# Feed-forward groups of five blocks instead of four in a pre-norm transformer block on one Trainium2 core

## The chip, the core and the metric

The kernel runs as one program on one core of one Trainium2 chip. The metric is the time of one execution on the device in microseconds (us). Three executions of the kernel before took 2558.55, 2560.4 and 2563.48 us, so the median is 2560.4 us. The arithmetic is float32 throughout.

Engines are named as the profile names them: PE multiplies matrices (its weight loads are shown as PEld), DVE is the vector engine, ACT the scalar engine, POOL the general one, and SP is the queue that issues nearly all DMA transfers. Each engine runs its own instructions in order and waits on the others through semaphores.

## The reference

The input x has 2048 rows (tokens) of 1024. The reference computes

```
x = x + attention(layernorm(x), wq, bq, wk, bk, wv, bv)   # 32 heads of 32, attention over the heads of each token
n = layernorm(x)
h = silu(n @ dq(w1).T) * (n @ dq(w2).T)                   # w1, w2: 2752 x 1024
x = x + h @ dq(w3).T                                      # w3: 1024 x 2752
```

where `dq` quantizes a weight to the 16 NF4 levels in blocks of 64 values, scaled by each block's largest absolute value, and expands it again. So every weight of the feed-forward part has to pass through `dq` inside the kernel. The 2752 hidden features are 21 blocks of 128 and a half block of 64. The code numbers them 0 to 21.

## The kernel before, in words

**Two halves.** The first part (up to some 840 us of the profile) projects q, k and v and computes the attention, in three sweeps over eight pairs of token tiles. The second part is the feed-forward. The products are built by a Strassen-like scheme: seven products stand in for eight. On the way, sums of operand tiles are kept in DRAM.

**The dequantization runs beside all this as a background job.** The list `jobs` holds one job for each weight block: kind "1" and "2" for the rows of w1 and w2, kind "3" for the columns of w3, kind "12" for the two half blocks together. There are 65 jobs. Their order follows `GROUPS`: for each group first the jobs "1" and "2" of all its blocks, then the jobs "3" of all its blocks. The generator `background()` cuts a job into steps, 17 for each job: 15 threshold steps (an ACT instruction into `sg`, L211, and a DVE instruction into `r`, L214 or L216), a step that takes the next job's absolute maxima (`am`, L184, with 16 small ACT multiplications into `wn`, L172), and a last step that scales `r` back. Once the feed-forward runs, every second job scales with one DVE instruction (L227), the others with 16 ACT multiplications (L172). A finished job then waits in `pending` for its transposes (`finish`): PE transposes it in two halves of four (`ptw`, L146), ACT copies each half to `wop` (L147), and for kinds 2, 12 and 3 an SP transfer stores the result in DRAM (`wd`, L159).

**How steps come into the program.** The order of PE's instructions is the order in which the code emits them. The order on the other engines is chosen by the framework's scheduler from readiness and program order. In the attention part, `advance(n)` emits n steps at fixed places. In the feed-forward, each product calls `spent`, which emits 0.67 steps for each nominal microsecond of PE work, and lets `flush(1)` emit one piece of transposing when the running job has reached its sixth step or later. Where a block is needed that isn't stored yet, `until` emits steps and transposes at once, without waiting for their turn:

```
def until(kind, c):
    while (kind, c) not in wd:
        if pending:
            flush(1)
        else:
            next(bg)
```

**The feed-forward.** Tokens are handled in two halves (`tbp` 0 and 1) of 1024. A pass is one group of blocks for one half. For each block of the group a `Unit` computes seven products (`mul`, each of four 128x128 by 128x512 matmuls and `spent(3.43)`), and makes from them two tiles `h`. The products run in the order first (one), middle (four), last (two), and the first product of the next unit is put between middle and last of the present one. Block 0 of half 0 is computed earlier, beside the end of the attention, by `plain_block`. After the middle of a group's last unit, `ask_w3(g)` loads the third weights of the group's blocks from DRAM into tiles of the pool `w3p`, through `load_w3`, which first calls `until("3", c)`:

```
if unit.c == min(g[-1], NFULL - 1):
    for c in [c for c in w3T if c not in g]:
        del w3T[c]
    ask_w3(g)
```

**The sums.** Then `down` multiplies the `h` of the group with the third weights: for each of 8 token tiles of the half and 2 column halves, one sum over the group's blocks grows in a PSUM bank (`po`, L924), and one DVE addition adds it to a running sum `acc` (L945). `acc` is loaded from DRAM (`x1d`) before and stored after, by SP; the last group stores to the output. Each `down` calls `spent(1.7 * len(full))` eight times. The passes go (g0, half 0), (g0, half 1), (g1, half 1), (g1, half 0) and so on, and the third weights stay for both passes of a group.

Of the kernel before, what the change touches and what calls it, by code (L numbers as in the profile page):

```python
# [12 lines left out]
FP = mybir.dt.float32  # L13
# [5 lines left out]
P = 128  # L19
# [10 lines left out]
NFULL = F // P  # L30
HALF = F - NFULL * P
TB = 512
NTBP = S // (2 * TB)
RATE = 0.67
XOPS = ("B11", "B12", "B21", "B22", "T1", "T2", "T3", "T4")
GROUPS = [list(range(g, min(g + 4, NFULL + 1))) for g in range(0, NFULL + 1, 4)]
BIG = float(2.0**100)

NF4_CODE = np.array(
# [19 lines left out]
def preln_block_kernel(  # L59
# [51 lines left out]
    jobs = []  # L111
    for g in GROUPS:
        for c in g:
# [135 lines left out]
    left, right = ExitStack(), ExitStack()  # L249
# [504 lines left out]
        advance(n)  # L754

    def new_h():
        return hp.tile([P, TB], FP, tag="h", name="h", bufs=10)

    def plain_block(c, tbp):

# [51 lines left out]
    tail.close()  # L812

    hp = ctx.enter_context(tc.tile_pool(name="hp", bufs=1, side="left", reuse_waits="tile"))
    w3p = ctx.enter_context(tc.tile_pool(name="w3p", bufs=5, side="left", reuse_waits="tile"))
    accp = ctx.enter_context(tc.tile_pool(name="accp", bufs=3, side="left", reuse_waits="tile"))
    ps_q = ctx.enter_context(
        tc.tile_pool(name="ps_q", bufs=2, space=PSUM, side="left", reuse_waits="tile")
# [12 lines left out]
    class Unit:  # L831
# [19 lines left out]
        def middle(self):  # L851
            q = self.q = ps_q.tile([P, TB], FP, tag="q", name="q")
            self.mul(7, q, True, False)
            self.mul(6, self.z, False, False)
            u2 = self.u2 = hp.tile([P, TB], FP, tag="u2", name="u2", bufs=2)
            nc.scalar.copy(u2, self.z)  # L856
            r = ps_r.tile([P, TB], FP, tag="r", name="rr")
            self.mul(2, r, True, True)
            nc.vector.tensor_tensor(self.g0, self.g0, r, ALU.add)
            nc.scalar.activation(self.g0, self.g0, AF.Silu)  # L860
            self.mul(5, self.z, False, False)
            u4 = hp.tile([P, TB], FP, tag="u4", name="u4")
            nc.scalar.copy(u4, self.z)
            self.h = [new_h(), new_h()]
            nc.vector.tensor_tensor(self.h[1], u4, q, ALU.add)
# [11 lines left out]
    class Half:  # L877


        def __init__(self, tbp):  # L880
            until("12", NFULL)
            self.tbp = tbp
            self.w = wT.tile([P, 7, 4, P], FP, tag="w12", name="w12h")
            nc.sync.dma_start(self.w[:, 0:2], wd["12", NFULL])
            self.si = hp.tile([P, TB], FP, tag="si", name="si")
            self.h = new_h()
# [21 lines left out]
    def down(g, tbp, hs):  # L908

        full = [c for c in g if c < NFULL]  # L910
        last = g is GROUPS[-1]
        for q in range(4):
# [42 lines left out]
    passes = []  # L955
    for n, g in enumerate(GROUPS):
        for tbp in (0, 1) if n % 2 == 0 else (1, 0):
# [68 lines left out]
```

## Time and profile before

| | before |
|---|---|
| median of three executions | 2560.4 us |
| the profiled execution | 2564.3 us |
| its span in the profile | 2562.5 us |
| PE, DVE, ACT busy | 2456.5, 2001.2, 1674.9 us |
| additions `acc` (L945) | 192, mean 682 ns |
| loads of `acc` from `x1d`, stores to `x1d` | 96, 80, of 512 KB each |
| mean granted PE clock | 0.982 |

The span runs from the first to the last instruction in the profile. The time of the execution, 2564.3 us, is 1.8 us longer and lies 3.9 us above the median. In a group's line of the profile, "x1344 | 599.4, 600 | 17.2" says that there are 1344 instructions, busy for 599.4 us, of mean 600 ns, and that the engine was idle for 17.2 us just before them. PE's instructions overlap: each float32 matmul of 128x512 is two records of some 0.6 us that start 0.43 us apart, so one `mul` is eight records and 3.43 us.

### The profile page before, as it was taken

To read this page: it belongs to the slowest core of one execution; us is meant where nothing else is said; L and a number is where in the kernel's file an instruction comes from. 1 tells how busy PE (TensorE), PEld (TensorE's weight loads), DVE (VectorE), ACT (ScalarE), POOL (GpSimd) and SP (SyncE) were. 2 spreads that over 40 slices of the span, in tenths; PEclk is the share of its full clock that TensorE was granted. 3 is DMA by queue.
4 is the path that set the end of the run, shared out by engine and by line. 5 is a ranking of instruction groups with operands and counts; after the bars stand their busy time and mean duration, and the time that the engine had idled before them with its cause. 6 is when DMAs were issued, how large, how long until landed. Compare 5 with 4: busy or idle time off the path is not lost.

```text
span 2562.5 us, 36651 instructions
## 1 busy us (share of the span) xinstructions
PE 2456.5 (96%) x14160; PEld 1151.3 (45%) x14160; DVE 2001.2 (78%) x2240; ACT 1674.9 (65%) x3190; POOL 31.6 (1%) x72
## 2 busy tenths in 40 slices
PE   8999899999998999999999999999999999999997
PEld 4444455544444444444444444444444444444433
DVE  7998788878898588888888888889888898871222
ACT  4657545445654478879788898888987978861000
POOL 1000000000000000000000000000000000000000
PEclk9999999999998999999999999999999999999999
DMA  8789533646677673364643546335365253641474
GB/s 301 290 308 353 205 140 131 243 166 211 219 241 268 224 265 133 136 221 156 246 144 136 197 156 263 144 122 219 123 252 187 107 209 134 231 184 62 149 280 142
DMA packets 156849, 506.03 MB, mean 197 GB/s; under 512 B 13633, under 2 KB 67905, under 8 KB 136833
## 3 DMA queue, kind: packets, MB, share of 16 engines
q1 hardware_dynamic: 156096, 503.63, 54.3%
q8 instruction: 111, 1.82, 0.3%
q14 instruction: 66, 0.53, 0.1%
q10 hardware_dynamic: 576, 0.05, 0.0%
HBM read 317.77 MB, written 185.86 MB: 197 GB/s over the span
## 4 chain that ended last, share of the span: by engine, by line
PE 24%; DVE 20%; ACT 17%; issue 6%; DMA 1%; DVEq 0%; SPq 0%
DVE r L216 16%; PE z L311 9%; PE po L924 9%; ACT sg L211 7%; ACT wn L172 5%; PE q L311 3%; ACT r L172 3%; PE rr L311 2%; ACT wop L147 1%; DVE acc L945 1%; PE po L936 1%; PE ptw L146 1%; DVE r L214 1%; DVE r L227 0%; ACT u L856 0%
## 5 line engine op out<-in xcount | busy, mean ns | idle before, releaser
L211 ACT ACTIVATE sg<-wn 128x1024 f32<-128x1024 f32 (+1 forms) x975 | 1012.0, 1048 | 304.7 <-DVE r L216 259.9
L216 DVE SCALAR_TENSOR_TENSOR r<-sg,r 128x1024 f32<-128x1024 f32 (+1 forms) x910 | 1104.2, 1213 | 113.5 <-ACT sg L211 75.5
L924 PE MATMUL po<-w,h 128*128 128x512 f32 x1344 | 599.4, 600 | 17.2 <-DVE acc L945 14.0
L924 PEld LDWEIGHTS po<-w,h 128*128 128x128 f32 x1344 | 251.8, 192 | 338.8 <-issue 289.6
L311 PE MATMUL z<-xB,w 128*128 128x512 f32 x720 | 323.3, 598 | 14.3 <-DMA w<-wd 12.0
L311 PE MATMUL z<-xT,w 128*128 128x512 f32 x656 | 297.2, 596 | 2.0 <-ACT u L856 1.9
L311 PE MATMUL q<-xT,w 128*128 128x512 f32 x656 | 291.0, 592 | 0.0
L172 ACT ACTIVATE wn<-wn,rc 128x64 f32<-128x64 f32 x1032 | 270.4, 336 | 26.6 <-DVE rc L192 26.6
L311 PEld LDWEIGHTS z<-xB,w 128*128 128x128 f32 x720 | 134.9, 192 | 175.4 <-issue 165.0
L945 DVE TENSOR_TENSOR acc<-acc,po 128x512 f32<-128x512 f32 x192 | 129.8, 682 | 107.2 <-PE po L924 64.9
L311 PE MATMUL z<-wB,A 128*128 128x512 f32 x384 | 186.3, 631 | 17.5 <-ACT u L329 17.3
L311 PEld LDWEIGHTS q<-xT,w 128*128 128x128 f32 x656 | 123.7, 190 | 151.3 <-issue 149.4
L311 PEld LDWEIGHTS z<-xT,w 128*128 128x128 f32 x656 | 123.0, 191 | 149.7 <-issue 140.6
L311 PE MATMUL z<-wT,A 128*128 128x512 f32 x384 | 181.4, 617 | 7.1 <-ACT u L329 4.5
L311 PE MATMUL q<-wT,A 128*128 128x512 f32 x384 | 173.1, 593 | 2.4 <-DVE A L364 1.5
L172 ACT ACTIVATE r<-r,am 128x64 f32<-128x64 f32 x608 | 152.4, 338 | 27.0 <-DVE r L216 27.0
L311 PE MATMUL rr<-xB,w 128*128 128x512 f32 x328 | 150.0, 601 | 0.0
L184 DVE TENSOR_REDUCE am<-wn 128x16 f32<-128x1024 f32 (+1 forms) x65 | 78.4, 1206 | 61.1 <-ACT r L172 55.8
L311 PEld LDWEIGHTS z<-wB,A 128*128 128x128 f32 x384 | 73.6, 201 | 100.9 <-issue 78.3
L311 PEld LDWEIGHTS z<-wT,A 128*128 128x128 f32 x384 | 72.4, 195 | 89.9 <-issue 81.7
L311 PEld LDWEIGHTS q<-wT,A 128*128 128x128 f32 x384 | 71.9, 190 | 90.0 <-issue 82.9
L856 ACT COPY u<-z 128x512 f32<-128x512 f32 x41 | 23.5, 573 | 131.6 <-PE z L311 131.6
(104 smaller groups left out, 1809.8 us busy)
## 6 DMA issues: line engine op xcount, KB each, us to landing
w<-wd SPq DMA_DIRECT2D x41, 1280.0 KB, 6.9
acc<-x1d SPq DMA_DIRECT2D x96, 512.0 KB, 3.5
wd<-wop SPq DMA_DIRECT2D x21, 2048.0 KB, 6.9
x1d<-acc SPq DMA_DIRECT2D x80, 512.0 KB, 2.9
wn<-in_w_dram SPq DMA_DIRECT2D x63, 512.0 KB, 4.1
w<-wd SPq DMA_DIRECT2D x62, 512.0 KB, 4.1
xT<-xdT SPq DMA_DIRECT2D x28, 1024.0 KB, 8.0
xB<-xdB SPq DMA_DIRECT2D x24, 1024.0 KB, 4.8
```

The costliest lines, as they stand in the source:

```text
L146: nc.tensor.transpose(pt[:q, k, :], v[:, j * q : (j + 1) * q], ident)
L147: nc.scalar.copy(o[:q, first + half], pt[:q])
L172: nc.scalar.mul(dst[:, ts(n, BLOCK)], src[:, ts(n, BLOCK)], by[:, n : n + 1])
L184: nc.vector.tensor_reduce(am[:, :nb], v.rearrange("p (b e) -> p b e", e=BLOCK), AX.X, ALU.max, apply_absolute_value=True,)
L211: nc.scalar.activation(t, v, AF.Copy, bias=EDGES[i], scale=BIG)
L214: nc.vector.tensor_scalar(r, t, code, -1.0, ALU.min, ALU.max)
L216: nc.vector.scalar_tensor_tensor(r, t, code, r, ALU.min, ALU.max)
L311: nc.tensor.matmul(dst, w[:, k, :], xop[:, k, :], start=start and k == 0, stop=stop and k == 3, skip_group_check=True,)
L856: nc.scalar.copy(u2, self.z)
L924: nc.tensor.matmul(po, hs[c][j][:, ts(q, P)], w3T[c][:, ts(n, 512)], start=(c == g[0]), stop=(c == g[-1]), skip_group_check=True,)
L936: nc.tensor.matmul(po, hs[NFULL][r, ts(q, P)], w3T[NFULL][r, ts(n, 512)], start=False, stop=True, skip_group_check=True,)
L945: nc.vector.tensor_tensor(a[:, ts(n, 512)], a[:, ts(n, 512)], po, ALU.add)
```

## The change

Groups have five blocks instead of four: 0 to 4, 5 to 9, 10 to 14, 15 to 19, and 20 with the half block 21, where before they were 0 to 3, 4 to 7, 8 to 11, 12 to 15, 16 to 19, and 20 with 21. That makes five groups and ten passes instead of six and twelve. The order of the background's jobs changes with the groups. A sum in PSUM runs over five blocks. The ring of `h` tiles has 12 buffers instead of 10, and the ring of third weights 6 instead of 5.

```diff
-GROUPS = [list(range(g, min(g + 4, NFULL + 1))) for g in range(0, NFULL + 1, 4)]
+GROUPS = [list(range(g, min(g + 5, NFULL + 1))) for g in range(0, NFULL + 1, 5)]
...
     def new_h():
-        return hp.tile([P, TB], FP, tag="h", name="h", bufs=10)
+        return hp.tile([P, TB], FP, tag="h", name="h", bufs=12)
...
-    w3p = ctx.enter_context(tc.tile_pool(name="w3p", bufs=5, side="left", reuse_waits="tile"))
+    w3p = ctx.enter_context(tc.tile_pool(name="w3p", bufs=6, side="left", reuse_waits="tile"))
```

## The prediction

> **What bounds the kernel now.** I read the page first, then the waits of the stretch 960 to 2200 us, then busy time by stage, then single waits in the timelines.
>
> ```profile
> PE 2456.5 (96%) x14160; PEld 1151.3 (45%) x14160; DVE 2001.2 (78%) x2240; ACT 1674.9 (65%) x3190; POOL 31.6 (1%) x72
> DVE  7998788878898588888888888889888898871222
> ACT  4657545445654478879788898888987978861000
> L945 DVE TENSOR_TENSOR acc<-acc,po 128x512 f32<-128x512 f32 x192 | 129.8, 682 | 107.2 <-PE po L924 64.9
> ```
>
> PE is busy 96% of the span, yet DVE and ACT stand at 8 or 9 tenths from slice 15 to slice 36: the feed-forward while weights are still being dequantized. After about 2300 us only PE works. Two things can therefore set the pace: PE's program, or the chain of DVE and ACT that makes the weights. The waits from 960 to 2200 us (total, times, longest) show which:
>
> ```profile
> ACT sg L211 <- DVE r L216: 137.7, 256, 2.1
> DVE r L216 <- ACT sg L211: 62.7, 59, 3.4
> DVE am L184 <- ACT r L172: 39.5, 18, 3.8
> DVE acc L945 <- PE po L924: 16.9, 10, 3.2
> PE po L924 <- DVE acc L945: 14.0, 11, 3.4
> PE ptw L146 <- DVE r L227: 11.8, 3, 6.4
> ```
>
> DVE and ACT wait for each other, hardly for PE. The scalings of every second job, from the view of tile r in that stretch, give the chain's pace:
>
> ```profile
> L227 DVE TENSOR_TENSOR r<-r,am x23: 1217/1219/1225, 982.1 to 2195.7; 128x1024 f32<-128x1024 f32 x23
> ```
>
> That is 22 intervals of two jobs in 1213.6 us: 27.6 us a job. PE's program advances a job each 17 steps, 17 / 0.67 = 25.4 us of nominal work; its 8 transposes start 0.11 us apart and add 0.9: 26.3 us. So the chain is the slower one by 1.3 us a job, and PE loses that in small waits. PE's start-to-start times beyond the regular 0.43 and 0.11 us sum to some 26 us in the downs and 24 us in the units that have background work. The last is the clearest (PE, DVE and ACT timelines):
>
> ```profile
> 2187.11 3.60 PE L311 MATMUL z<-xT,w 128*128 128x512 f32 x8
> 2197.10 1.09 PE L146 MATMUL ptw<-ident,r 128*128 128x128 f32 x4 [6.39 <-DVE r L227]
> 2197.98 6.09 PE L311 MATMUL rr<-xB,w 128*128 128x512 f32 x8
> ```
> ```profile
> 2195.73 1.22 DVE L227 TENSOR_TENSOR r<-r,am 128x1024 f32<-128x1024 f32 x1
> ```
> ```profile
> 2167.59 3.93 ACT L172 ACTIVATE r<-r,am 128x64 f32<-128x64 f32 x16
> ```
>
> PE waits 6.39 us for job 61's scaling, which ends at 2196.95; the job before it, 60, ended at 2171.52 on ACT. From 2197.10 on PE has 365.4 us to the end of the span, no longer bound by the chain.
>
> **What the change removes.** One group less is two passes less: 32 additions of 0.682 us (21.8 us of DVE), 32 loads and 32 stores of 512 KB. PE's matmuls stay: 1344 records of po either way. One set of operand loads goes too. The DMAs are worth nothing directly: acc lands in 3.5 us, and DVE waited for it 2.0 us in the stretch. What they cover is PE's time, so I count only the additions, through the chain. The additions also hold PSUM banks that PE wants (14.0 us above, some more at the weight loads); with five blocks a pair of sums takes 8.6 us of PE instead of 6.9, so each bank has more time to come free. That belongs to the same chain and isn't counted twice. The larger rings match the group: 10 tiles of h and 2 for the next unit, 5 third weights and one spare, as 8 and 2, 4 and 1 before. No cost, unless they were smaller.
>
> **What it moves: the deadline of the last third weight.** Job k is complete at step 17k + 1. By the code the attention emits 8 x 7 + 8 x 8 + 8 x 9 = 192 steps, the plain block 3: 195.
> - Before: the first request for third weights comes after 19 products: 195 + 19 x 3.43 x 0.67 = 238 steps. Job 12 needs 205: 33 in hand. A cycle of two passes emits (56 x 3.43 + 2 x 8 x 6.8) x 0.67 = 201.6 and needs 12 x 17 = 204. So 31, 28, 26 and 24 are in hand at the next four requests, and `until` never emits anything.
> - After: the first request comes after 26 products: 195 + 59 = 254 steps. Job 15 needs 256. A cycle emits (70 x 3.43 + 2 x 8 x 8.5) x 0.67 = 252 and needs 255. So each of four requests is 2 to 3 steps short: `until` emits them and both halves of the transposes at once, in front of PE's next product. A slack of 24 to 33 steps (36 to 49 us) becomes none, four times.
>
> The parts of this wait: (a) PE stands until the job is scaled. (b) Between the two halves PE waits for ACT's copy, since `ps_tr` has one buffer; I take 2.5 us with the transposes (0.45 each), bounds 1.5 to 4: copies of 0.57 us followed the transposes by up to 2.4 us in the trace. (c) Then copy, store and load of that third weight: about 2 + 3.1 + 4.1 (the medians to landing) + 0.7 for two issues = 9.9 us, beside one product of the next unit, two of this one and 3.4 us of the first sum = 13.7 us. Covered, with 3.8 us to spare. The next unit's weights don't queue behind it: SP's order follows readiness (the trace issues a third weight as soon as it is stored, 31 us before its down). Queued behind the wait on PE is everything; on ACT the copy of the next unit's first product.
>
> **The sum.** At the first request the chain is ahead (the neighbouring job 14 was ready 14 us before PE reached its point), so only (b) counts. At the fourth, job 60 decides. The PE work left there: 3 products in the stage, a down of 20 product-lengths, 35 products, a down of 20 = 78 before the last group. At 2197.10 in the trace there are 5 + 16 + 28 + 16 = 65. The difference is 13 x 3.43 = 44.6 us. So
> end = T60 + 3.5 (release, both halves, copy) + 44.6 + 365.4 - 2.5 (the slow matmuls at 2197.98: 6.09 instead of 3.60) = T60 + 411.0.
> T60 was 2171.5. What shifts it: 32 additions less by that point (6 downs instead of 8), credit between 0 (ACT is the bound) and 21.8; I take three quarters, 16.4, because in the downs DVE is nearer to full than ACT (this stage, from the busy times by stage: DVE 52.56 and ACT 45.31 of 57.70):
>
> ```profile
> 1401.80:1459.50 57.70, 56.98 (x142) 25.14 (x141) 52.56 (x61) 45.31 (x84) 0.00 (x0) 1.00 0.56 205
> ```
>
> About 1.1 units more by then (33.7 against 32.6) x 5 DVE operations of 0.684 = +3.8. DVE and ACT starved for part of (b) at the second and third request: 0 to 4 us each, I take 1.5: +3. So T60 = 2161.9, and the end 2572.9.
> Plus the clock. After the gaps of 6.4 us here, 4.0 at 1977.1, 3.2 at 1278.7 and 3.5 at 1603.1, four to eight matmul records started 0.85 us apart instead of 0.43: 1.6 to 3.1 us lost; after one of 3.5 at 1767.7, none. One such loss lies behind the last decisive wait (earlier ones are absorbed by the next wait for the chain): +3, bounds 0 to 3.1. Span 2576, which is +13.5; from the profiled execution 2564.3 that is 2578, from the median, 3.9 lower, 2574.
>
> [...]
>
> **Range of the forecast.** Full credit, no starving, no clock loss: T60 = 2153.5, end 2564.5, +2: 2562. No credit, 4 us twice, the dearer (b) and clock: T60 = 2183.3, end 2599, +36: 2597.
>
> **Rivals.**
> 1. *Faster.* The additions are the bound, and with them gone the weights are ready when asked: the chain gains on PE. Then the waits of 26 us in downs halve, the 16 us behind late scalings (waits of 1.7, 4.0 and 6.4, and slow matmuls) go, and four times (b) is paid: -13 - 16 + 10 = -19, 2541. For it: DVE above 90% in downs. Against: ACT has the same 65 jobs and DVE waits for it 102 us. It decides if job 60 is done at or before PE arrives: PE passes that place at about 2144 before (ten products after the down that ends at 2107.5), so T60 would have to fall by 28 us; the additions hold 21.8, and the chain would have to lose its waits for PE (16.9 us) as well.
> 2. *No change.* The saving and the late deadline cancel: the low end above with some of the 26 us regained. 2560.
> 3. *Much slower.* The last third weight lands late. With the longest landings of these rows (11.7 for a store, 7.6 for a load) path (c) is 22 us, 8.2 over its cover, four times: 2574 + 33 = 2607. Against: medians of 3.1 and 4.1.
>
> **Chances.** Forecast 0.68, rival 1 0.14, rival 2 0.10, rival 3 0.08. The measurement tells 0.2%, 5 us, from no change. Of the forecast's range a small part, 0.03, lies within that: faster 0.14, same 0.13, slower 0.73. To hold 8 in 10 the range takes the forecast and rival 2, and reaches halfway to rival 3: 2559 to 2600.
>
> **What would show it.** Four PE waits at ptw, at about 930, 1340, 1750 and 2165 us, the first short, the later ones of 5 to 25 us with DVE r or ACT r as releaser, each followed by the last w3 load; 160 additions; fewer waits po <- acc; background done by about 2285; after the fourth wait PE without gaps. Wrong: if those waits are under 3 us (rival 1), or if PE waits at po for w3 loads (rival 3), or if job 60 ends after 2171.

## The result and the profile after

The change makes the kernel slower. Five executions of the kernel after gave a median of 2620.07 us (2618.62 to 2627.45), beside 2561.93 us for the kernel before in the same comparison: a ratio of 1.0239, 95% interval 1.0226 to 1.0253, or 58 us. The direction was forecast. The size, +13.5 us, was not, and 2620 lies above the range of 2559 to 2600. The profiled execution took 2620.07 us, its span is 2618.3 us (before 2562.5), the mean granted PE clock 0.972 (before 0.982).

From the profile's page of the kernel after: busy time by engine, the slices of DVE and ACT, and three groups (busy and mean ns, then the idle time just before them and what ended most of it).

```profile
PE 2466.4 (94%) x14160; PEld 1160.5 (44%) x14160; DVE 1987.5 (76%) x2208; ACT 1681.1 (64%) x3190; POOL 31.7 (1%) x72
DVE  7998778889886677887888888788788788751122
ACT  4658545545444776887987797898788798751000
L945 DVE TENSOR_TENSOR acc<-acc,po 128x512 f32<-128x512 f32 x160 | 108.0, 681 | 146.4 <-PE po L924 103.5
L146 PE MATMUL ptw<-ident,r 128*128 128x128 f32 (+1 forms) x520 | 89.3, 291 | 70.5 <-DVE r L227 31.5
L147 ACT COPY wop<-ptw 128x512 f32<-128x512 f32 (+1 forms) x130 | 74.8, 578 | 82.6 <-PE ptw L146 82.5
```

The 32 additions are gone, with the 21.8 us of DVE that were counted. The work is the same otherwise, but DVE and ACT now dip to 7 tenths and below again and again where before they stood at 8 and 9. Both lines of transposing have changed most: PE is idle 70.5 us before its transposes (L146), where before it was 12.8, and ACT 82.6 before its copies (L147; before 51.4), waiting for PE. The same two lines of the kernel before, and its ACT's wait for transposes from 960 to 2320 us:

```profile
L146 PE MATMUL ptw<-ident,r 128*128 128x128 f32 (+1 forms) x520 | 78.8, 275 | 12.8 <-DVE r L227 11.8 <-ACT wop L147 1.0
L147 ACT COPY wop<-ptw 128x512 f32<-128x512 f32 (+1 forms) x130 | 74.2, 573 | 51.4 <-PE ptw L146 51.2
ACT wop L147 <- PE ptw L146: 11.1, 5, 3.2
```

The waits of the stretch 960 to 2320 us, which holds the feed-forward with background work, show the pair in the kernel after (some lines left out):

```profile
ACT sg L211 <- DVE r L216: 149.5, 319, 1.5
DVE r L216 <- ACT sg L211: 63.6, 60, 3.2
...
DVE acc L945 <- PE po L924: 45.4, 25, 4.0
ACT wop L147 <- PE ptw L146: 38.7, 14, 8.4
...
PE ptw L146 <- DVE r L227: 31.5, 5, 10.7
PE ptw L146 <- ACT wop L147: 21.2, 7, 4.0
...
PE ptw L146 <- ACT r L172: 12.9, 11, 8.4
DVE r L214 <- PE ptw L146: 9.7, 3, 3.3
```

Two things are to be seen. `PE po <- DVE acc`, 14.0 us before, is gone: a bank does have more time to come free. And there is a loop that the kernel before did not have at this size: ACT and DVE wait for PE's transposes (`wop <- ptw`, 38.7 us where it was 11.1, and `r` L214 `<- ptw`, the first instruction of a new job, which before had no such wait after 1000 us), while PE waits for their scalings.

The timeline of PE shows how. First one down of the kernel after, then the next pass, to the place where PE stops.

```profile
1149.55 25.91 PE L924 MATMUL po<-w,h 128*128 128x512 f32 x60
1175.30 0.60 PE L146 MATMUL ptw<-ident,r 128*128 128x128 f32 x4
1175.74 8.75 PE L924 MATMUL po<-w,h 128*128 128x512 f32 x20
1184.32 0.60 PE L146 MATMUL ptw<-ident,r 128*128 128x128 f32 x4
1184.76 25.92 PE L924 MATMUL po<-w,h 128*128 128x512 f32 x60
1210.51 0.60 PE L146 MATMUL ptw<-ident,r 128*128 128x128 f32 x4
...
1259.50 3.60 PE L311 MATMUL z<-xB,w 128*128 128x512 f32 x8
1273.81 1.09 PE L146 MATMUL ptw<-ident,r 128*128 128x128 f32 x4 [10.71 <-DVE r L227]
1274.69 5.87 PE L311 MATMUL z<-xB,w 128*128 128x512 f32 x8
```

In 70 us PE transposes three halves, 1.5 jobs. DVE in the same place:

```profile
1211.37 1.23 DVE L227 TENSOR_TENSOR r<-r,am 128x1024 f32<-128x1024 f32 x1
...
1219.73 0.69 DVE L945 TENSOR_TENSOR acc<-acc,po 128x512 f32<-128x512 f32 x1 [3.60 <-PE po L924]
1223.68 0.69 DVE L214 TENSOR_SCALAR r<-sg 128x1024 f32<-128x1024 f32 x1 [3.26 <-PE ptw L146]
```

A job is scaled at 1212.60. The next one's first threshold is ready on ACT at 1212.42, but both buffers of `r` hold finished jobs, one half transposed and one not at all, so DVE can start it (L214) only at 1223.68, after the transposes at 1222.97. For 11.1 us the chain makes no threshold: DVE has 3.7 us of additions and small steps, ACT 4.5 us of a copy and of the small multiplications into `wn`. That job ends at 1249.8, 37.2 us after the one before it, and the one after that at 1273.7. PE has run out of other work at 1263.1 and waits 10.71 us for it. The chain loses 11 us in the down, where PE has plenty to do, and PE pays them in the next pass.

The cause is a count in the code; the experiments below test it. `down` calls `spent` eight times, whatever the group's size, and each call gives `flush(1)` one turn at most. With five blocks those eight calls emit 8 x 8.5 x 0.67 = 46 steps, 2.7 jobs, which need 5.4 halves of transposing; with four, 36 steps, 2.1 jobs, 4.3 halves, and three or four were transposed. The pile that was small with four blocks grows past what two buffers of `r` can hold.

### The profile page after: what moved, and what is told of

Same layout as the page of the kernel before. It is cut to its first block, busy times and chain, and to the rows that moved or that the text cites. A ratio compares the mean times of both kernels' runs of the same rounds, so it can differ in the third digit from the quotient of the medians.

```text
span 2618.3 us, 36524 instructions
## 1 busy us (share of the span) xinstructions
PE 2466.4 (94%) x14160; PEld 1160.5 (44%) x14160; DVE 1987.5 (76%) x2208; ACT 1681.1 (64%) x3190; POOL 31.7 (1%) x72
## 4 chain that ended last, share of the span: by engine, by line
PE 39%; DVE 15%; ACT 11%; issue 3%; DMA 2%; DVEq 0%; SPq 0%
PE po L924 21%; DVE r L216 12%; PE z L311 10%; PE q L311 5%; ACT sg L211 5%; ACT wn L172 3%; ACT r L172 2%; PE rr L311 2%; PE ptw L146 1%; DMA out_dram<-acc 1%; DMA acc<-x1d 1%; ACT wop L147 1%; DVE r L214 0%; DVE am L184 0%; DVE r L227 0%
## 5 line engine op out<-in xcount | busy, mean ns | idle before, releaser
L924 PE MATMUL po<-w,h 128*128 128x512 f32 x1344 | 585.9, 594 | 2.8 <-DVE h L871 2.8
L311 PE MATMUL z<-xB,w 128*128 128x512 f32 x720 | 335.3, 615 | 13.3 <-DMA w<-wd 11.9
L311 PE MATMUL q<-xT,w 128*128 128x512 f32 x656 | 298.4, 606 | 0.3 <-DVE acc L945 0.3
L172 ACT ACTIVATE wn<-wn,rc 128x64 f32<-128x64 f32 x1032 | 268.7, 336 | 37.2 <-DVE rc L192 37.2
L945 DVE TENSOR_TENSOR acc<-acc,po 128x512 f32<-128x512 f32 x160 | 108.0, 681 | 146.4 <-PE po L924 103.5
L146 PE MATMUL ptw<-ident,r 128*128 128x128 f32 (+1 forms) x520 | 89.3, 291 | 70.5 <-DVE r L227 31.5
L146 PEld LDWEIGHTS ptw<-ident,r 128*128 128x128 f32 (+1 forms) x520 | 66.7, 147 | 140.6 <-issue 45.4
L147 ACT COPY wop<-ptw 128x512 f32<-128x512 f32 (+1 forms) x130 | 74.8, 578 | 82.6 <-PE ptw L146 82.5
```

What stands on the lines that cost most here:

```text
L146: nc.tensor.transpose(pt[:q, k, :], v[:, j * q : (j + 1) * q], ident)
L147: nc.scalar.copy(o[:q, first + half], pt[:q])
L172: nc.scalar.mul(dst[:, ts(n, BLOCK)], src[:, ts(n, BLOCK)], by[:, n : n + 1])
L311: nc.tensor.matmul(dst, w[:, k, :], xop[:, k, :], start=start and k == 0, stop=stop and k == 3, skip_group_check=True,)
L924: nc.tensor.matmul(po, hs[c][j][:, ts(q, P)], w3T[c][:, ts(n, 512)], start=(c == g[0]), stop=(c == g[-1]), skip_group_check=True,)
L945: nc.vector.tensor_tensor(a[:, ts(n, 512)], a[:, ts(n, 512)], po, ALU.add)
```

## The experiments

The main theory is this pile-up: too few turns of `flush` in a down fill the ring `r` and stop the chain. Rival A is the prediction's own mechanism at a larger price: the requests for third weights that `until` forces are the loss. All ratios are to the kernel before in the same comparison, with 95% intervals. Medians come from several comparisons, in which the kernel before had 2556.3 to 2561.9 us, so runs are compared by their ratios. T60 is the time at which job 60 is scaled, as in the prediction; a job's pace is taken from job 21 to job 61.

| run | blocks | median us | ratio | T60 | us a job |
|---|---|---|---|---|---|
| before | 4 | 2560.4 (three executions) | | 2171.5 | 27.6 |
| after | 5 | 2620.1 | 1.0239 [1.0226, 1.0253] | 2198.9 | 28.1 |
| e1_after_flush | 5 | 2562.6 | 1.0007 [0.9995, 1.0018] | 2143.2 | 27.0 |
| e2_before_rare | 4 | 2643.5 | 1.0325 [1.0303, 1.0347] | 2251.6 | 29.2 |
| e3_rings | 4 | 2561.2 | 1.0004 [0.9990, 1.0018] | 2167.5 | 27.6 |
| e4_before_flush | 4 | 2561.9 | 0.9998 [0.9984, 1.0012] | 2165.7 | 27.4 |
| e5_flush_lead | 5 | 2562.8 | 1.0015 [1.0004, 1.0026] | 2127.3 | 27.1 |
| e6_lead | 5 | 2601.4 | 1.0160 [1.0140, 1.0180] | 2178.1 | 28.0 |
| e7_r3 | 5 | 2568.0 | 1.0035 [1.0022, 1.0047] | 2144.8 | 27.3 |
| e9_fewer_adds | 4 | 2550.6 | 0.9966 [0.9954, 0.9978] | 2159.6 | 27.4 |
| e10_flush_rate | 5 | 2562.1 | 1.0022 [1.0011, 1.0032] | 2128.1 | 26.8 |
| e11_flush_r3 | 5 | 2551.8 | 0.9985 [0.9977, 0.9994] | 2120.3 | 27.1 |
| e12_before_r3 | 4 | 2549.5 | 0.9971 [0.9959, 0.9983] | 2134.7 | 27.5 |
| e13_all | 5 | 2547.3 | 0.9963 [0.9950, 0.9975] | 2098.8 | 26.8 |

**e1_after_flush: five blocks, and one more turn of `flush` in the middle of each pair of sums.**

```diff
                     pos.append(po)
+                    if len(pos) == 1 and step["n"] in range(5, 15):
+                        flush(1)
```

> Groups of five as changed; between the two sums of each pair in down, one more call of flush(1) under the same condition as in spent. By the order of emission a down then carries 4 halves of transposes instead of 3, and never more than one finished job waits for its transposes (2 in the changed kernel). Theory (transposes pile up in the longer downs, the two buffers of r stop the chain of DVE and ACT, and PE pays for it in the next pass): the waits of 9 to 11 us early in the passes that follow a down go, 35 to 55 us of the loss of 58 us go with them, 2565 to 2585 us; the four requests for third weights still cost. Rival A (the four forced requests are the loss): within 8 us of 2620. Rival B (the chain is slower for another reason, and the place of the waits means nothing): within 8 us of 2620 too, with the waits moved elsewhere.

The ratio is 1.0007 [0.9995, 1.0018], 2562.6 us: this one added turn takes the whole loss away, a little more than the 35 to 55 us expected, and rivals A and B, by which the time stays near 2620, fall. The timeline of PE in a down of e1 has four halves where the kernel after has three, and the next unit follows with no stop (lines left out):

```profile
1165.17 0.60 PE L146 MATMUL ptw<-ident,r 128*128 128x128 f32 x4
...
1169.94 0.60 PE L146 MATMUL ptw<-ident,r 128*128 128x128 f32 x4
...
1192.76 0.60 PE L146 MATMUL ptw<-ident,r 128*128 128x128 f32 x4
...
1197.49 0.60 PE L146 MATMUL ptw<-ident,r 128*128 128x128 f32 x4
```

And in its waits from 960 to 2320 us ACT's wait for transposes falls from 38.7 to 8.3 us, DVE's for the sums from 45.4 to 8.7, and `DVE r L214 <- PE ptw` is gone:

```profile
DVE acc L947 <- PE po L924: 8.7, 8, 4.0
ACT wop L147 <- PE ptw L146: 8.3, 4, 6.8
```

**e2_before_rare: groups of four, with four turns of twice the steps in a down instead of eight.**

```diff
-                spent(1.7 * len(full))
+                if n:
+                    spent(3.4 * len(full))
```

> Groups of four as before; down spends its steps once for two pairs of sums (3.4 instead of 1.7 for each), so flush(1) is called four times in a down instead of eight. Same steps, same sums, same deadlines, no forced request; a down carries 1 to 3 halves instead of 3 or 4, and 2 to 3 finished jobs wait. Theory of the pile-up: slower than before by 30 to 70 us, with waits of PE at ptw early in the passes after a down, as in the changed kernel. Rivals A and B: within 6 us of before.

The steps emitted in a down stay the same, and so do groups, additions and rings; only turns are fewer. The ratio is 1.0325 [1.0303, 1.0347], a larger loss than the change's, and more than the 30 to 70 us expected, with the same signature in its waits from 960 to 2320 us:

```profile
ACT wop L147 <- PE ptw L146: 65.8, 11, 23.2
PE ptw L146 <- DVE r L227: 23.9, 5, 8.6
```

So the loss needs no group of five. e1 takes it out of five blocks, e2 puts it into four.

**e3_rings: groups of four with the larger rings (12 `h`, 6 third weights).**

```diff
-        return hp.tile([P, TB], FP, tag="h", name="h", bufs=10)
+        return hp.tile([P, TB], FP, tag="h", name="h", bufs=12)
...
-    w3p = ctx.enter_context(tc.tile_pool(name="w3p", bufs=5, ...
+    w3p = ctx.enter_context(tc.tile_pool(name="w3p", bufs=6, ...
```

> Groups of four as before, only the rings of h (12) and of third weights (6) enlarged. All theories: within 4 us of before; more would mean that the place of the tiles in memory or their release matters.

1.0004 [0.9990, 1.0018]: the rings by themselves cost and bring nothing that can be measured.

**e4_before_flush: groups of four with the added turn of e1.**

> Groups of four as before, with the additional flush(1) between the two sums of a pair. A down carries 4 halves always, and at most one finished job waits (2 in some downs before). Theory of the pile-up: 0 to 10 us faster than before, since some downs of before pile up too. Rivals: within 3 us of before.

0.9998 [0.9984, 1.0012]. The turn is worth nothing where turns suffice, though job 60 is done 5.8 us earlier. So e1 does not hide another loss behind a general gain of the added turn. DVE's wait `r L214 <- ptw` is there too, 7.5 us in six short waits, and the time is no longer than before: this wait alone does not tell a loss.

**e7_r3: the kernel after with a third buffer of `r`.** The pile of untransposed jobs stays; only the ring that it fills is larger. To make room the attention's tile `xU` has two buffers instead of three, and there are five third weights.

```diff
-            r = dqp.tile([P, E], FP, tag="r", name="r", bufs=2)[:, :w]
+            r = dqp.tile([P, E], FP, tag="r", name="r", bufs=3)[:, :w]
...
-            u[n + 1] = work.tile([P, 4, P], FP, tag="xU", name="xU", bufs=3)
+            u[n + 1] = work.tile([P, 4, P], FP, tag="xU", name="xU", bufs=2)
```

> Groups of five as changed, with three buffers of r instead of two, so that the chain can finish one more job while transposes pile up; to make room the ring xU in the attention has 2 buffers instead of 3 and the ring of third weights 5 instead of 6. If the two buffers of r are what stops the chain: 25 to 45 us faster than the changed kernel (2575 to 2595 us); waits of PE for ACT's copies between adjacent transposes remain. If the pile-up costs through those adjacent transposes alone (one buffer of wop, one PSUM bank): within 8 us of 2620.

2567.97 us, 1.0035 [1.0022, 1.0047]: about 50 of 58 us come back, more than I expected. In its waits PE no longer waits for DVE's scalings at all, while it still waits for copies at the places where halves come one after the other:

```profile
PE ptw L146 <- ACT wop L147: 26.8, 9, 5.7
ACT wop L147 <- PE ptw L146: 18.3, 5, 7.9
```

So the link between few turns and lost time is the ring: piled-up transposes cost little as long as the chain can go on. The other reading, by which the adjacent transposes alone are the cost, asked for a time within 8 us of 2620 and falls.

**e12_before_r3: the same third buffer with groups of four.**

> Control: groups of four as before with three buffers of r (and xU 2). Theory (at most two finished jobs wait in four downs of before, one elsewhere): 0 to 6 us faster than before. If three buffers help any such kernel by tens of us, then e7_r3 did not show the cause: 15 us or more faster.

2549.54 us beside 2556.32, 0.9971 [0.9959, 0.9983], some 7 us. That is the control for e7: the third buffer alone is worth an eighth of what it brings to five blocks, although it puts the chain 34 us ahead by job 21 (1058.5 beside 1092.2 us; in e7 26 us ahead of the kernel after).

**e6_lead: the kernel after with 24 more steps emitted at the end of the attention, so that no request for third weights is short.**

```diff
-    advance(2)
+    advance(10)
...
-    advance(1)
+    advance(9)
+    flush()
...
+    advance(8)
+    flush()
```

> Groups of five as changed, with the 24 steps in hand of e5_flush_lead but without the additional flush(1): no request is forced, transposes pile up as in the changed kernel (3 or 4 halves in a down, two finished jobs waiting). Theory of the pile-up: 10 to 25 us faster than the changed kernel, 2595 to 2610 us, so most of the loss stays. Rival A (the forced requests are the loss): 2570 us or less.

2601.36 us, 1.0160 [1.0140, 1.0180]: about 20 of the 58 us. Rival A, by which the forced requests are the loss, falls. The chain stops as in the kernel after (ACT waits 48.7 us for transposes in the same stretch, 38.7 there). The lead costs something itself: PE waits 6.55 and 4.72 us at the end of the attention, so that the forced requests and the lead together may be worth up to some 11 us more than the 20. The parts of the loss do not simply add up: e1 wins back all 58 with the forced requests in place.

**e5_flush_lead: e1 with the same 24 steps.**

> Groups of five with the additional flush(1) of e1_after_flush, and 24 more background steps at the end of the attention: beside the plain block advance(10), advance(9), advance(8), each with flush(), in place of advance(2) with flush(), and advance(1). Then the first request for third weights has 22 steps in hand, the next ones 19, 16 and 13, and none is forced. Theory (the forced requests still cost some 20 us in e1_after_flush: waits of 3.0, 3.4, 4.4 and 3.4 us between the halves or for the scaling, with slow matmuls after three of them): 12 to 22 us faster than e1_after_flush, 2541 to 2551 us. Rival (the chain of DVE and ACT sets the end, and forced waits only show where PE meets it): within 5 us of e1_after_flush.

2562.78 us, 1.0015 [1.0004, 1.0026], no faster than e1, where the forced requests still cost PE four waits of 3 to 4 us. The 12 to 22 us expected did not come. Job 60 is done 15.9 us earlier (2127.3), but the end does not follow: PE loses time at the end of the attention (waits of 6.57 and 4.58 us at 847.0 and 861.0), where the steps now stand.

**e10_flush_rate: e1 with a higher rate of steps until the first third weights are loaded.** This moves the lead into the first units instead.

```diff
-RATE = 0.67
+RATE = 0.68
...
-        owed += us * RATE
+        owed += us * (RATE if w3T else 0.84)
```

> Groups of five with the additional flush(1) of e1_after_flush; RATE 0.68 instead of 0.67, and 0.84 until the first third weights are loaded. The first request then has 13 steps in hand, the next 14, 15 and 16, and none is forced; the steps are taken from the first pass, where the chain was 15 us ahead, not from the end of the attention, where e5_flush_lead lost some 14 us. Theory (the forced requests cost about 20 us that e5_flush_lead gave back at the attention's end): 8 to 18 us faster than e1_after_flush, 2544 to 2554 us. Rival (the chain sets the end whatever the requests do): within 5 us of e1_after_flush.

1.0022 [1.0011, 1.0032], again no faster. From 960 to 2320 us the waits at `ptw` are about as in e1 (11.7 us in all, 14.0 there), released by scalings where they were released by copies, and PE now waits 13.8 us for ACT's copies `u` (in e1 6.3). Removing the forced waits shifted them. The 8 to 18 us expected did not come here either; in both runs the rival's forecast, within 5 us of e1, holds by the ratios. That the chain sets the end is not shown by that: job 60 is done some 15 us earlier in both, and the time does not follow.

**e9_fewer_adds: groups of four, without the 32 additions of the third group,** which prices the additions.

```diff
-                for (i, j, a), po in zip(at, pos):
+                for (i, j, a), po in zip(at, pos) if g is not GROUPS[2] else ():
```

> Groups of four as before; the 32 additions of the third group's sums to acc are left out, so that group's part is missing from the output, while its sums, its loads and stores of acc stay. This prices the additions alone. The prediction's credit of three quarters: the chain is 16 us ahead by the end, and 10 to 16 us less time. If ACT is the bound, or if the additions lie beside other work: within 3 us of before.

2550.58 us beside 2559.62, 0.9966 [0.9954, 0.9978]: 9.0 us for 21.8 us of DVE, with job 60 earlier by 11.9, each a little under what was expected (10 to 16 and 16 us). With the additions some of PE's waits for a PSUM bank go too (`PE po <- DVE acc`, 14.0 us before, 7.0 here), so the price holds both.

**e11_flush_r3 and e13_all: what five blocks reach once all is mended.** e11 is e1 with the third `r` of e7; e13 adds the rates of e10.

> Groups of five with the additional flush(1) and with three buffers of r (xU 2, third weights 5, as in e7_r3). Theory (one finished job waits at most once the flush is added, so two buffers do): within 6 us of e1_after_flush, 2557 to 2568 us. If the ring of r holds the chain in other places too: 8 us or more faster.

> Groups of five with the additional flush(1), three buffers of r and the rates of e10_flush_rate: the candidate for the fastest. Theory: the better of e10_flush_rate and e11_flush_r3 or up to 5 us below it, 2540 to 2554 us. Rival (the chain sets the end): within 5 us of e1_after_flush.

0.9985 [0.9977, 0.9994] and 0.9963 [0.9950, 0.9975]. By the ratios e11 is some 6 us faster than e1, at the edge of the 6 us expected, which does not decide between the two readings; e13, which has no forced request, is by as much faster than e11. The best version with five blocks, e13 at 2547.3 us, and the best with four, e12 at 2549.5, have overlapping intervals. Both beat the two kernels by little. That five blocks by themselves bring anything is not shown.

## Why the prediction was wrong

**The step that failed is T60.** The forecast took 2171.5, subtracted 16.4 for the additions, added 3.8 and 3, and came to 2161.9. Measured was 2198.9, 37 us later. The sum's only terms for a slower chain were more units by then (+3.8) and starving at the forced requests (+3). It had none for the chain's stopping because its results are not taken away: that term was put at nothing, and one such stop, in one down, is 11 us long. I had worked out how many steps a cycle emits and had not counted the turns of `flush` beside them, though the front of this document says that `spent` lets `flush(1)` emit one piece. "Wrong: if job 60 ends after 2171" was the test that caught it, and e1, e2 and e7 name what is behind it.

**The formula behind it held where PE waits for job 60.** End = T60 + 411.0 gives 2609.9 with the measured T60; the span is 2618.3. Of the 8.4 us, 6.8 are a wait of 4.03 us at 2308 and the slow matmuls and transposes after it, which lie behind the place that the prediction called the last decisive one. In e1, where the pile-up is gone, T60 is 2143.2, the formula gives 2554.2 plus the clock term, and the span is 2556.3. Where job 60 comes earlier still, PE no longer waits for it and the formula gives too little: e13 has T60 at 2098.8, the formula 2509.8, the span 2545.5.

**The moved deadline was real, and its price was paid elsewhere.** By the formula a given T60 ends 20 us later with five blocks than before (411.0 against 2562.5 - 2171.5 = 391.0). Between e4 and e1, four and five blocks with the same added turn, T60 is 22.5 us earlier and the time the same. So what the larger groups save in the chain was worth about the deadline. Without the missed term the answer would have been near rival 2, no change, and for its reason: saving and deadline cancel. Of the 22.5 us the additions explain some 11.9, by e9; where the rest comes from no run shows.

**The additions** were credited with 16.4 us. e9 gives 11.9 at T60 and 9.0 us of time: about half of the 21.8, not three quarters. That they count through the chain alone fits these figures, but e9 does not separate the chain from the shorter waits for PSUM banks.

**The forced requests** came where they were forecast. PE's timeline at the second of them, after:

```profile
1348.72 0.81 PE L146 MATMUL ptw<-ident,r 128*128 128x128 f32 x2 [0.73 <-ACT r L172]
1350.15 0.80 PE L146 MATMUL ptw<-ident,r 128*128 128x128 f32 x2 [0.63 <-ACT r L172]
1353.01 1.11 PE L146 MATMUL ptw<-ident,r 128*128 128x128 f32 x4 [2.05 <-ACT wop L147]
```

The other three are at 932.5 (2.79 us, the copy between the halves only, as forecast), 1776 and 2199. By PE's start-to-start times their waits are some 4.7, 7.3 and 4.7 us where 5 to 25 were expected, with some 2.5 us of slow transposes and matmuls behind each. Together the four cost PE some 27 us of the 119 that its start-to-start times lose in the feed-forward (before 61). The difference of 58 covers the whole loss. The larger part, some 66 us, lies in the waits behind the downs: 10.71, 8.45 and 10.72 us at 1273.8, 1694.5 and 2120.1, four of 4.0 us about 1039, 1462, 1885 and 2308, and the slow matmuls after each. Smaller waits for transposes make some 14 us, and after 2450 us 13 are lost, as before (11). The prediction named no wait behind the downs.

**Path (c)** was covered, as forecast: the downs with their 160 records and transposes take 70.0 us without a stop, and in no down does PE wait for a load, so no third weight landed late, and rival 3 falls. Rival 1, faster, falls with T60, and e1 shows that even with T60 28 us earlier than before, the amount that it asked for, the time is only level. The forced requests still hold PE up for 3 to 4 us each there, but e5 and e10, which have none, are no faster.

**The background's end** was forecast for about 2285. The last threshold runs at 2289.6 before, 2329.4 after and 2260.4 in e1.

**The clock** was taken as one loss of at most 3.1 us. After, each of the waits of 4.0 us and more is followed by slow matmuls. The first and the last of these, PE's timeline:

```profile
1038.92 1.12 PE L146 MATMUL ptw<-ident,r 128*128 128x128 f32 x4 [4.02 <-ACT wop L147]
1039.83 8.98 PE L311 MATMUL q<-xT,w 128*128 128x512 f32 x16
...
2308.23 1.12 PE L146 MATMUL ptw<-ident,r 128*128 128x128 f32 x4 [4.03 <-ACT wop L147]
2309.14 7.05 PE L311 MATMUL q<-xT,w 128*128 128x512 f32 x11
```

Sixteen records took 8.98 us where undisturbed they take 7.03, and four transposes 1.12 where they take 0.60: some 2.5 us a gap. The granted clock of the same profile was 0.76 from 1038.92 to 1048.81 us and 0.59 to 0.76 in the 7 to 10 us behind each of the seven waits; in the undisturbed down from 1149.5 to 1219.5 it was 1.00.

## What to carry to other kernels

Where side work gets its turn from the emission of other work, count turns as well as amounts: for each unit of the main work, how many pieces the side work produces, how many turns it has to be taken away, and how many buffers hold the difference. A change that enlarges the unit can leave every amount in proportion and still halt the producer, and the price then shows later, on another engine, as a wait for something that was late. Adding one turn, or one buffer to the ring, is a cheap test and was here worth 50 to 58 us.

## What was not expected of the hardware

The length of a gap alone did not decide here whether slow matmuls followed it. After a gap of 2.79 us (932.5, after) ten records took 4.46 us, as undisturbed; after one of 3.23 us (2146.05, e1) sixteen records took 8.17 instead of 7.03; after one of only 1.91 us (1788.90, e9) eight took 5.40 instead of 3.60. Longer gaps hardly cost more: after 10.71 us eight records took 5.87 instead of 3.60, 2.3 us, and after 4.02 us it was 2.0.

The granted clock in the profiles goes with this. Behind the gap of 2.79 us it was 1.00 (932.5 to 937.0 us, after), behind that of 10.71 us 0.60 (1273.81 to 1280.56). Three more stretches read as follows (from:to, us, then PE, PEld, DVE, ACT and POOL busy, the granted PE clock, the DMA share and GB/s). First e9 behind its gap of 1.91 us, then the kernel before, behind the gap of 3.2 us at 1278.7 and behind that of 3.5 us at 1767.7, after which the prediction had found no loss:

```profile
1790.14:1793.55 3.41, 3.41 (x5) 1.33 (x4) 3.31 (x4) 3.14 (x4) 0.00 (x0) 0.50 0.39 137
```
```profile
1278.72:1284.99 6.27, 6.27 (x8) 2.67 (x9) 4.12 (x4) 2.55 (x3) 0.00 (x0) 0.52 0.57 184
1767.67:1771.37 3.70, 3.70 (x10) 1.74 (x11) 3.49 (x4) 3.70 (x13) 0.00 (x0) 1.00 0.34 142
```

Behind the two shorter of these gaps the granted clock was about half, 0.50 and 0.52, and behind the longest it was 1.00. What sets it back, these rows do not show.
